# One attention stage: scores of the next head pair ahead of other stages' work, and one reciprocal for two query tiles

## The chip, the cores and the metric

The kernel runs on one core of a Trainium2 chip. The core has a matrix engine (TensorE, PE in the profile; its weight loads are PEld), a vector engine (VectorE, DVE), a scalar engine (ScalarE, ACT), a general engine (GpSimd, POOL) and a queue engine for transfers (SyncE, SP). Each takes its instructions in the order in which they were written for it; semaphores tie the engines together. The metric is the device time of one execution in microseconds (us), the median of several runs.

## The reference, cut to what matters

The program is a chain of four blocks ("macaron": half a feed-forward layer, attention, half a feed-forward layer) on 8 x 512 tokens of 128 features, all in float32. The stage that is changed is the attention of the third block, called L2:

```python
def _L2_attn_ref(x, Wq, Wk, Wv, Wo, bo):
    B, N, D, H, DH = (2, 256, 128, 16, 64)
    b, n, _ = x.shape
    scale = DH ** (-0.5)
    q = (x @ Wq).reshape(b, n, H, DH)
    ...
    bias = slope[:, None, None] * (pos[:, None] - pos[None, :])
    scores = jnp.einsum('bihd,bjhd->bhij', q, k) * scale + bias[None]
    causal = pos[:, None] >= pos[None, :]
    scores = jnp.where(causal[None, None], scores, jnp.float32(-1e+30))
    attn = jax.nn.softmax(scores, axis=-1)
    out = jnp.einsum('bhij,bjhd->bihd', attn, v).reshape(b, n, H * DH)
    return out @ Wo + bo
```

In the chain it stands between two feed-forward layers; the last of L1 and the first of L3 run beside it:

```python
    x = x + 0.5 * _L1_ffn_ref(_layernorm(x, axis=-1), ...)
    x = x + 0.5 * _L2_ffn_ref(_layernorm(x, axis=-1), ...)
    x = x + _L2_attn_ref(_layernorm(x, axis=-1), ...)
    x = x + 0.5 * _L2_ffn_ref(_layernorm(x, axis=-1), ...)
    x = x + 0.5 * _L3_ffn_ref(_layernorm(x, axis=-1), ...)
```

The batch is 8 here, the sequence 512 and there are 16 heads of 64 features.

## The kernel before

`l2_block` (L1642) handles one pair of heads of one batch element at a time; such a pair is called a unit. There are 8 batches x 8 pairs = 64 units, numbered n. The 512 queries of a unit are four tiles i = 0 to 3 of 128 queries. As attention is causal, tile i has 128 (i + 1) keys, and its probabilities stand side by side in one row of 1280 columns from the offsets `OFF`.

For a unit these steps are done, each by a small function that issues instructions and often returns the ACT part to be issued later:

- `project(n)` (L1668): two matmuls give queries and keys of both heads (`pp`), ACT copies them to SBUF (`qk`, L1676), negated and scaled.
- `values(n, half)` (L1679): the value matmuls (`vp`, L1687) and DVE's copy `v` (L1688).
- `score(n, i)` (L1696): one score matmul for each head (`s`, L1706); DVE adds the bias and takes the row minimum in one pass (L1710; as queries are negated, the minimum is the maximum); ACT takes the exponential and, in the same pass, the row sum (L1713). The sum goes to column i of the little tile `sums[n]`.
- `norm(n, *tiles)` (L1736): for each tile named, DVE takes the reciprocal of the two heads' sums (L1740) and multiplies both heads' probabilities (L1743).
- `turn(n, m)` (L1721): PE transposes four 128 x 128 blocks of probabilities (`tp`, L1732), ACT copies them out (`pt`, L1734). Five such calls make up a unit.
- `weigh(n)` (L1745): eight matmuls of probabilities and values (`o`, L1757) and ACT's copy `att` (L1760).
- `leave(b)` (L1762), once for each batch: the output projection (`op`, L1766) and the update of x.

Other stages' work runs in the same loop. `plan` (L331) puts its steps under numbers in the table `todo`, and `works(at)` (L1800) issues what stands under a number. Unit n calls `works(3n)`, `works(3n + 1)` and `works(3n + 2)`: phases 0, 1 and 2. By the numbers given, phase 1 has:

- the update of the two L2 feed-forward steps (`op`, L348, and DVE's `x`, L351; POOL adds the bias);
- the transposes of normalised x for the next batch's projections (`pt`, L314; copy `xta`, L321);
- of the L1 feed-forward layer: the router scores `sp` (L1048), ACT's copy `q` (L1049) and the gelu with its activation table (L1054, L1055), whose next step (L1060 to L1063, ending in ACT's `comp`) is in phase 2; one step each of a long chain of small DVE operations (L1087 to L1091; L1111 to L1115 and L1126); the spline (`pa`, L1138; ACT's copy L1145; eight DVE operations L1148 to L1155), whose next step (a second `pa` and ACT's L1163) is in phase 2;
- of the L3 feed-forward layer: the transposes `pt` with ACT's copy `xt` (L314, L321), whose next step, the routing logits `lp` (L366), is in phase 2; and three of the eight expert steps (`yp`, L384, and four updates of x by DVE, L386);
- one projection of the L3 attention (L1932) with its transfers to and from HBM, and its values (L1953).

In this text a unit is named after such a work: the gelu unit, the route unit, the spline unit, the expert units, the pick unit (L1111 to L1126) and the turn unit (the transposes for the next batch's projections).

PE, ACT and DVE run in the order of the calls in the loop (L1811 on); nothing reorders them. PSUM is split in two: the score tiles `s` have two buffers, and everything else in the loop (`bank`, L1663) shares four buffers named "mm". Which of the four a tile takes is settled when the program is built; a tile's first matmul waits until the last reader of the buffer's former tile is done. In each unit the order is:

1. three of the five `turn` calls of unit n - 1, `project(n + 1)`, `score(n, 2)`, `score(n, 1)`; ACT's copies and exponentials of these and of the two scores that were begun in the unit before are then interleaved;
2. the last two `turn` calls, `norm(n, 3, 0)`, `works(3n)`, `values`, perhaps `leave`;
3. these lines (L1833 to L1843):

```python
                    if two:
                        weigh(n - 2)
                    if here:
                        norm(n, 2, 1)
                    works(3 * n + 1)
                    if -1 <= n and n + 1 < last:
                        late = score(n + 1, 3)
                        late += score(n + 1, 0)
                    if -3 <= n < 5:
                        slopes(n + 3)
                    works(3 * n + 2)
```

`slopes` (L1690) makes the bias of two heads on DVE, in the first units only. The exponentials in `late` are issued in the next unit, after the copies of the first two `turn` calls.

## Time and profile before

| what | value |
|---|---|
| median of 3 runs | 2609.69 us (2609.08 to 2613.6) |
| the profiled execution | 2632.98 us |
| its span, first to last instruction | 2631.2 us |
| mean granted TensorE clock | 0.960 |
| PE busy, share of the span | 2389.5 us, 91% |
| DVE busy | 2024.7 us, 77% |
| ACT busy | 1756.3 us, 67% |
| POOL busy | 1154.0 us, 44% |
| first and last score matmul of the stage (L1706) | 1014.0 and 1848.0 us |

The profile is of one execution, which with profiling on took a little longer than the runs. The span is the time from its first to its last instruction. "Busy" adds up an engine's instructions; matmuls overlap, and their ends are modelled. A row of a time line has the start, the length, the engine, the line of the program, the operation, out<-in by the program's names, the shape and the count of merged instructions; in brackets stands how long the engine had been idle before it and what ended that. A row of the list of groups has busy time and mean length, then the idle time before these instructions. A row of the list of waits has the total, the number and the longest.

### The profile page before, as it was taken

What the parts mean: (1) busy time and instruction counts of PE and PEld (TensorE: products, weight loads), DVE (VectorE), ACT (ScalarE), POOL (GpSimd) and SP (SyncE); (2) the same over time, 40 slices, a digit from 0 to 9 for tenths busy, and PEclk for the clock granted to TensorE, in tenths of its full rate; (3) what the DMA queues carried; (4) which work ended last, traced back from release to release, by engine and by line L of the source; (5) the groups of instructions that cost most, each with busy time, mean ns of one, the idle gap of its engine ahead of it and who ended that gap; (6) DMA issues with size and microseconds to landing.
All of it is one profiled execution on the core that took longest, in us unless ns stands there. A gap on an engine that the chain in (4) does not pass through costs nothing.

```text
span 2631.2 us, 51301 instructions
## 1 busy us (share of the span) xinstructions
PE 2389.5 (91%) x18184; PEld 1427.7 (54%) x18184; DVE 2024.7 (77%) x5597; ACT 1756.3 (67%) x4393; POOL 1154.0 (44%) x2003
## 2 busy tenths in 40 slices
PE   6858756999999998999999999999899999999997
PEld 6537533344444444566565655556565666666664
DVE  5347348888888866878788787877688989898897
ACT  2135134466677666766757676676598999999984
POOL 5655643244454452163452635332234545454443
PEclk9878877799999999999999999999899999999999
DMA  8121340001010100000000000000000000000000
GB/s 270 51 81 30 93 124 1 18 18 27 19 26 19 34 2 4 1 1 1 1 1 1 1 1 1 1 1 9 9 18 9 10 22 22 10 14 22 22 2 13
DMA packets 72962, 66.51 MB, mean 25 GB/s; under 512 B 15675, under 2 KB 62787, under 8 KB 70563
## 3 DMA queue, kind: packets, MB, share of 16 engines
q1 hardware_dynamic: 68096, 54.88, 7.7%
q0 software_dynamic: 3584, 7.58, 1.0%
q8 instruction: 145, 2.38, 0.4%
q10 hardware_dynamic: 1026, 0.78, 0.1%
q14 instruction: 111, 0.90, 0.1%
HBM read 36.47 MB, written 26.80 MB: 24 GB/s over the span
## 4 chain that ended last, share of the span: by engine, by line
PE 62%; DVE 20%; ACT 9%; POOL 4%; issue 3%; DMA 1%; another core or an unknown queue 0%; SPq 0%; POOLq 0%; DVEq 0%; ACTq 0%
PE tp L1476 8%; PE s L1450 6%; PE s L1290 5%; PE o L1757 4%; PE o L1492 4%; PE o L1320 4%; PE s L1706 4%; PE yp L384 3%; ACT e L1713 3%; PE s L1310 3%; DVE nm L1291 3%; DVE nm L1454 3%; PE tp L1732 2%; PE pp L1674 2%; PE hp L684 2%
## 5 line engine op out<-in xcount | busy, mean ns | idle before, releaser
L1461 ACT ACTIVATE e<-s,nm 128x512 f32<-128x512 f32 x512 | 345.4, 689 | 26.0 <-DVE nm L1454 21.4
L1291 DVE TENSOR_REDUCE nm<-s 128x2 f32<-128x1024 f32 x256 | 301.4, 1218 | 75.9 <-PE s L1310 61.0
L1454 DVE TENSOR_REDUCE nm<-s 128x2 f32<-128x1024 f32 x256 | 301.0, 1217 | 29.6 <-PE s L1450 27.7
L1482 ACT ACTIVATE p<-tp 128x512 f32<-128x512 f32 x512 | 279.3, 618 | 61.6 <-PE tp L1476 61.6
L1312 ACT ACTIVATE pr<-s 128x512 f32<-128x512 f32 x512 | 271.6, 600 | 73.1 <-PE s L1310 69.3
L1476 PE MATMUL tp<-cst,e 128*128 128x128 f32 x2048 | 294.3, 282 | 15.2 <-DVE rs L1467 7.9
L1476 PEld LDWEIGHTS tp<-cst,e 128*128 128x128 f32 x2048 | 221.5, 142 | 153.0 <-issue 86.8
L1470 POOL TENSOR_SCALAR e<-e,rs 128x512 f32<-128x512 f32 x114 | 200.1, 1755 | 229.8 <-DVE rs L1467 191.3
L1290 PE MATMUL s<-k,q 32*128 32x512 f32 x1024 | 279.2, 657 | 18.0 <-DVE nm L1291 14.6
L1310 PE MATMUL s<-q,k 32*128 32x512 f32 x1024 | 290.4, 627 | 5.4 <-DVE at L1333 4.4
L1713 ACT ACTIVATE e<-e,m 128x512 f32<-128x512 f32 (+3 forms) x512 | 286.1, 570 | 12.6 <-DVE m L1710 12.5
L1710 DVE CUSTOM_DVE_ANT_0 e<-s,bias 128x512 f32<-128x512 f32 (+3 forms) x512 | 220.1, 485 | 92.9 <-PE s L1706 92.4
L219 POOL TENSOR_TENSOR d<-st 128x4 f32<-128x4 f32 (+3 forms) x90 | 19.7, 218 | 554.2 <-DVE st L215 356.9
L1734 ACT COPY pt<-tp 128x512 f32<-128x512 f32 x320 | 174.5, 590 | 90.1 <-PE tp L1732 90.1
L386 DVE SCALAR_TENSOR_TENSOR x<-yp,sel,x 128x128 f32<-128x128 f32 x512 | 177.9, 348 | 39.7 <-PE yp L384 26.6
L1470 DVE TENSOR_SCALAR e<-e,rs 128x512 f32<-128x512 f32 x398 | 195.5, 521 | 9.1
L1743 DVE TENSOR_SCALAR e<-e,rc 128x512 f32<-128x512 f32 (+3 forms) x512 | 190.0, 416 | 9.1
L1732 PE MATMUL tp<-cst,e 128*128 128x128 f32 x1280 | 170.9, 278 | 9.8 <-ACT pt L1734 4.0
L1450 PE MATMUL s<-k,q 32*128 32x512 f32 x1024 | 174.8, 651 | 5.1 <-ACT e L1461 2.6
L1706 PE MATMUL s<-qk 64*128 64x512 f32 (+3 forms) x1024 | 173.6, 457 | 2.0 <-DVE m L1710 1.4
L1492 PE MATMUL o<-p,va 128*32 128x128 f32 x4096 | 165.8, 277 | 2.9 <-ACT p L1482 2.9
L1732 PEld LDWEIGHTS tp<-cst,e 128*128 128x128 f32 x1280 | 139.2, 141 | 48.5 <-issue 13.3
(467 smaller groups left out, 4848.0 us busy)
## 6 DMA issues: line engine op xcount, KB each, us to landing
yd<-z SPq DMA_DIRECT2D x8, 1024.0 KB
r<-yd SPq DMA_DIRECT2D x32, 256.0 KB
sk<-pu SPq DMA_DIRECT2D x16, 256.0 KB
k<-sk SPq DMA_DIRECT2D x60, 64.0 KB
w<-in_l_w SPq DMA_DIRECT2D x14, 256.0 KB
xd<-wqkv SPq DMA_DIRECT2D x12, 256.0 KB
x<-in_x SPq DMA_DIRECT2D x8, 256.0 KB
up<-in_l_up SPq DMA_DIRECT2D x8, 256.0 KB
```

The lines of the kernel that those rows point to most:

```text
L1290: nc.tensor.matmul(s[:, jj, :], lhsT=q[cut, g, i * P : (i + 1) * P], rhs=k[cut, g, :], start=True, stop=True)
L1291: nc.vector.tensor_reduce(nms[b, g // 2][:, i, 2 * h : 2 * h + 2, g % 2], s, AX.X, ALU.max, negate=True)
L1310: nc.tensor.matmul(s, lhsT=k[cut, g, kt * P : (kt + 1) * P], rhs=q[cut, g, :], start=True, stop=True)
L1450: nc.tensor.matmul(s[:, jj, :], lhsT=q[cut, g, i * P : (i + 1) * P], rhs=k[cut, g, :], start=True, stop=True)
L1454: nc.vector.tensor_reduce(nm, scores[n, h], AX.X, ALU.max, negate=True)
L1461: nc.scalar.activation(e, s[:, jj, :], AF.Exp, bias=nm[:, jj : jj + 1], accum_out=sm[:, jj : jj + 1])
L1470: (nc.gpsimd if h and jj and n >= 14 else nc.vector).tensor_scalar(e, e, rc[:, jj : jj + 1], None, ALU.mult)
L1476: nc.tensor.transpose(tp[:, kt, :], probs[n][j][:, kt * P : (kt + 1) * P], self.ident)
L1482: nc.scalar.activation(p, turns[n].pop(0), AF.Exp)
L1706: nc.tensor.matmul(s[:, jj, 0:w], lhsT=qs[n][cut, i * P : (i + 1) * P], rhs=ks[n][cut, 0:w], start=True, stop=True)
L1713: outs.append(lambda e=e, jj=jj: nc.scalar.activation(e, e, AF.Exp, bias=mins[n][:, jj, i : i + 1], scale=-1.0, accum_out=sums[n][:, jj, i ...
L1732: nc.tensor.transpose(tp[:, k, :], block(n, jj, i, kt), self.ident)
```

## The change

Two things are changed in `l2_block`.

The row sums of a unit no longer stand in the order of the tiles but as `SUM` says: tiles 3, 0, 2, 1 in columns 0 to 3. So the two tiles of each `norm` call stand next to each other, and one reciprocal over 2 heads x 2 tiles takes the place of two over 2 heads each. The multiplications stay as they are.

In the third part of a unit, `norm(n, 2, 1)` is written ahead of `weigh(n - 2)`, and the two scores of the next unit ahead of `works(3n + 1)`. So the order becomes: normalise, weigh, the next unit's two scores (matmuls and minima), other stages' work of phase 1, slopes, other stages' work of phase 2.

```diff
-        OFF = (0, 128, 384, 768)
+        OFF, SUM = (0, 128, 384, 768), (1, 3, 2, 0)
...
-                        e, e, AF.Exp, bias=mins[n][:, jj, i : i + 1], scale=-1.0, accum_out=sums[n][:, jj, i : i + 1]))
+                        e, e, AF.Exp, bias=mins[n][:, jj, i : i + 1], scale=-1.0, accum_out=sums[n][:, jj, SUM[i] : SUM[i] + 1]))
...
             def norm(n, *tiles):
 
-                for i in tiles:
-                    rc = wk.tile([P, 2], F32, tag="rc", name="rc", bufs=4)
-                    nc.vector.reciprocal(rc, sums[n][:, :, i])
+                rc = wk.tile([P, 2, 2], F32, tag="rc", name="rc", bufs=4)
+                nc.vector.reciprocal(rc, sums[n][:, :, SUM[tiles[0]] : SUM[tiles[0]] + 2])
+                for k, i in enumerate(tiles):
                     for jj in range(2):
                         e = es[n][:, jj, OFF[i] : OFF[i] + P * (i + 1)]
-                        nc.vector.tensor_scalar(e, e, rc[:, jj : jj + 1], None, ALU.mult)
+                        nc.vector.tensor_scalar(e, e, rc[:, jj, k : k + 1], None, ALU.mult)
...
+                    if here:
+                        norm(n, 2, 1)
                     if two:
                         weigh(n - 2)
-                    if here:
-                        norm(n, 2, 1)
-                    works(3 * n + 1)
                     if -1 <= n and n + 1 < last:
                         late = score(n + 1, 3)
                         late += score(n + 1, 0)
+                    works(3 * n + 1)
                     if -3 <= n < 5:
                         slopes(n + 3)
                     works(3 * n + 2)
```

## The prediction

> **What bounds the kernel now.** I read the page first (busy time by engine), then busy time in a window around the changed stage, then its waits, then the time line of TensorE (PE), ScalarE (ACT) and VectorE (DVE) over the eight units from 1353.1 to 1464.1 us. The stage's first score matmul is at 1014.0 us and its last at 1848.0; I take 1010 to 1860. Only there does the order change: on POOL and SP, and on every engine before and after this stage, the built programs have the same instructions in the same order.

> Window view; the columns are length, then busy us of PE, its weight loads, DVE, ACT, POOL:

> ```profile
> 1010.00:1860.00 850.00, 809.92 (x4803) 495.68 (x4802) 671.92 (x2596) 597.55 (x1665) 339.51 (x745) 1.00 0.01 3
> ```

> PE is idle for 850.00 - 809.92 = 40.1 us, DVE for 178.1, ACT for 252.5. The matmuls stand end to start, so PE sets the pace, and all that a better order can bring here is part of those 40.1 us. A new order of PE's own work costs nothing in itself; it costs where PE then has to wait.

> The stage repeats every eight units: the output projection (L1766) comes at 1242.21, 1353.14, 1464.07, 1575.00, 1685.95, so a period is 110.9 us. PE's time line in one period ("idle before" in brackets, with its releaser):

> ```profile
> 1382.99 1.12 PE L1674 MATMUL pp<-xta,wqkv 128*128 128x512 f32 x2 [1.07 <-ACT pt L1734]
> ...
> 1414.61 0.66 PE L314 MATMUL pt<-cst,xn 128*128 128x128 f32 x4
> 1415.19 1.35 PE L1706 MATMUL s<-qk 64*128 64x512 f32 x8
> 1416.47 1.06 PE L366 MATMUL lp<-gw,xt 128*128 128x8 f32 x8
> ...
> 1431.53 1.35 PE L1706 MATMUL s<-qk 64*128 64x384 f32 x8 [0.23 <-DVE m L1710]
> 1434.20 0.44 PE L1131 MATMUL tp<-cst,k 128*128 128x128 f32 x2 [0.30 <-ACT qk L1676]
> 1436.35 2.37 PE L1757 MATMUL o<-pt,v 128*64 128x512 f32 x16 [0.54 <-ACT pt L1734]
> ...
> 1444.71 0.66 PE L1732 MATMUL tp<-cst,e 128*128 128x128 f32 x4 [0.41 <-ACT k L1163]
> ...
> 1458.06 1.98 PE L1674 MATMUL pp<-xta,wqkv 128*128 128x512 f32 x4
> ```

> The same period on ACT:

> ```profile
> 1378.41 0.40 ACT L1049 COPY q<-sp 128x288 f32<-128x288 f32 x1 [1.42 <-PE sp L1048]
> 1378.82 1.28 ACT L1055 ACT_TABLE_LOAD   x1
> 1380.12 0.31 ACT L1055 ACTIVATE q<-q 128x128 f32<-128x128 f32 x1
> 1381.98 0.49 ACT L1063 ACTIVATE comp<-q,cb 128x4 f32<-128x4 f32 x2 [1.55 <-DVE q L1061]
> ...
> 1415.38 0.61 ACT L321 ACTIVATE xt<-pt 128x512 f32<-128x512 f32 x1
> ...
> 1430.90 0.72 ACT L1713 ACTIVATE e<-e,m 128x512 f32<-128x512 f32 x1 [1.14 <-DVE m L1710]
> ...
> 1443.52 1.15 ACT L1163 ACTIVATE k<-pa,q 128x128 f32<-128x128 f32 x4 [2.88 <-PE pa L1138]
> ```

> And DVE (the expert updates L386 and the reciprocals are what to look at):

> ```profile
> 1455.00 0.15 DVE L1740 RECIPROCAL rc<-sm 128x2 f32<-128x2 f32 x1
> 1455.18 0.65 DVE L1743 TENSOR_SCALAR e<-e,rc 128x256 f32<-128x256 f32 x2
> 1455.76 1.50 DVE L386 SCALAR_TENSOR_TENSOR x<-yp,sel,x 128x128 f32<-128x128 f32 x4
> 1457.17 0.68 DVE L1710 CUSTOM_DVE_ANT_0 e<-s,bias 128x512 f32<-128x512 f32 x1
> ```

> **Prices used throughout.** A pair of score tiles holds PE for 1416.47 - 1415.19 = 1.28 us. DVE can begin its four minimum passes (L1710) 1.18 us after the scores start (1378.24 to 1379.42 in the gelu unit) and they take 1.64 (1443.08 to 1444.72, the next start). Four expert updates take 1.42 to the next start, 1.50 to their end.

> **The change, part by part.**

> *Reciprocals.* 256 of 0.159 us become 128; each new one covers twice the columns (by the 128x32 one of L1088, 0.353, two more columns are about 0.013). DVE is spared 256 x 0.159 - 128 x 0.172 = 18.7 us, nearly all beside PE's work: DVE already waits 92.4 us for score matmuls. It reaches the path where PE waits for a normalised tile: 1.87 and 1.21 us at 1022.7 and 1031.9 and 0.57 at 1853.1, each shortened by two omitted instructions of 0.19 (0.15 and its gap, rows above): -1.1 us. The joint reciprocal waits for the later of two exponentials; where that binds (after 1390.3, the first pair was scaled while the second was awaited) DVE is 0.8 late, to 1393.25, but the scores it reads next are not there before 1393.67.

> *Normalising ahead of weighing.* One is DVE's, the other PE's and ACT's: the order on no engine changes. Nothing.

> *Scores ahead of the other stages' work.* Every such work of phase 1 comes 1.28 us later on PE and 1.64 later on DVE; the minima come earlier by what stood before them. Unit by unit:

> Route unit (1412 on). Before, the scores stood between the transposes pt and the routing matmuls lp, and hid the copy xt. Now pt starts at 1414.61 + 1.28 = 1415.89, the copy 0.77 after it as before (1415.38 - 1414.61), ends at 1417.27, and lp starts at about 1417.3 instead of 1416.47: +0.8. Behind lp on PE stand the next unit's transposes, on which ACT waits. Seven such units; in the last one L1953's vp (1.0 us) stands between, as the cover: 6 x 0.8 = +4.8.

> Gelu unit (1374 on). The router scores sp come 1.28 later, so copy q, table load and gelu end at 1380.43 + 1.28 = 1381.71. L1060 and L1061 used to wait for the minima (until 1381.07), and now for gelu; with 0.46 + 0.42 and the gaps comp starts at 1382.65 instead of 1381.98. The pt copies stand behind comp, and PE's 1.07 wait is for them: +0.67. From there ACT is continuous to the wait at 1390.18, so nothing gives it back. 6 x 0.67 = +4.0.

> Pick unit and spline unit (1424, 1436). In the first, the minima no longer stand behind six instructions of L1111 to L1126; ACT's 1.14 wait goes and with it PE's 0.23 + 0.30 + 0.54 = 1.07. In the second the direction: scores now at 1437.58 (1438.65 - 1.07), minima from 1438.76 to 1440.40, updates to 1441.82, the spline's eight (1.76) to 1443.58. ACT's L1163 needs the last of them: 1443.62, it was 1443.52. So the pair gives back what it gains: +0.1, six times: +0.6. Without the first unit's gain it would be +1.2 each.

> Expert units. In the changed program the unit's first projection pp takes a PSUM buffer that the first expert update still reads; 18 units have such a wait, none before (transposes and later tiles had it). Around 1458: DVE is free 0.38 sooner, at 1455.38; minima to 1457.02, update to 1458.52, pp at 1458.58 instead of 1458.06: +0.5, 6 x = +3.0. In the third of the three units (1366) the same sum ends at 1366.94, before pp's 1367.17: nothing, with 0.2 to spare. In the first (spline) the update ends with the transposes.

> Turn unit (1401). PE's 0.14 wait goes, six times: -0.8.

> Other moved work is covered: x L351 is read next 1.8 us later at 1396.22 and ends at 1396.1; the projection at 1830.03 sends its transfer 1.28 later, but that of the other half, whose source is ready only at 1841.54, is the later one anyway. POOL's operations stay in their order and wait 245.9 us for DVE already.

> **Sum.** 4.8 + 4.0 + 0.6 + 3.0 - 1.1 - 0.8 = +10.5 us. The profiled execution took 2632.98 us (span 2631.2), 23.3 above the median of the runs, 2609.69; I add the same to both: span about 2641.7, time 2620. From both sides, each term: route 0 to 5.6; gelu 0 to 4.0; pick and spline -6.4 (all of 1.07, nothing late) to 7.2 (6 x 1.2); experts 0 to 5.6 (0.5 plus the 1366 unit's margin missed by 0.4); gains -3 to 0.

> [...]

> **Rivals.**
> 1. Faster, one mechanism: the earlier minima free ACT in the pick unit, and the spline's chain does not bind. For it: ACT's 12.5 us of waiting for minima. Against: the spline's last result (L1155, to 1443.17) comes only 0.35 us before L1163 starts. It pays -6.4 - 1.1 - 0.8 = -8.3 and decides if route, gelu and experts together lose less than that, as when PE's later waits absorb them: 2601.
> 2. No change: PE's work is the same and gains meet losses: 2610. For it: 95% busy; against: waits now exposed are not among the old ones.
> 3. Slower still: the pick unit gains nothing and all bank waits bite: 5.6 + 4.0 + 7.2 + 5.6 = 22 us, 2632. Against: DVE has six instructions fewer before those minima.

> **How the numbers follow.** The forecast 0.55, rival 3 0.10, rival 2 0.16, rival 1 0.19. This kernel's measurement tells 0.2%, 5.2 us, from no change. So faster 0.19, same 0.16, slower 0.65. The forecast's own range is 2615 to 2626; across the cases 2602 to 2631.

> **What would show it.** Route unit: lp with an idle time of 0.8 before it, for ACT xt. Gelu unit: the second pp waiting 1.7. Pick unit: no waits at L1706, L1131, L1757. Expert unit: pp waiting 0.5 for DVE x. PE's idle time in the stage near 51 us, not 40; 128 reciprocals. It is wrong if PE's idle time falls, or if the time moves outside this stage.

## The result and the profile after

| what | before | after |
|---|---|---|
| median of the runs beside each other | 2610.15 us | 2618.6 us |
| ratio | | 1.0039, 95% interval 1.0030 to 1.0048 |
| first to last score matmul of the stage | 833.98 us | 843.41 us |
| stage, from first to last weighing | | +9.25 us |
| DVE busy in the execution | 2024.7 us | 2006.2 us |

The change makes the kernel 8.45 us slower by the medians, 0.3% to 0.4%. (The ratio is not formed from the medians, whose quotient is 1.0032; its interval holds both.) The profiled execution of after has the shorter span (2612.4 us), because the part ahead of the stage happened to take 26 us less in it: the first score matmul comes at 987.7 us and not at 1014.0. So only the stage is compared below.

Busy time in a window around the stage, columns as before (length; PE, its weight loads, DVE, ACT, POOL):

```profile
984.00:1834.00 850.00, 796.83 (x4750) 494.69 (x4751) 649.52 (x2450) 588.35 (x1649) 339.00 (x745) 0.99 0.01 3
```

PE is now idle for 850.00 - 796.83 = 53.2 us (40.1 before), and DVE has less to do. The waits of PE in that window, after (what waited and for what; total, times, longest):

```profile
PE pp L1674 <- ACT pt L1734: 16.1, 6, 3.0
PE tp L1732 <- ACT k L1163: 9.8, 5, 2.0
PE o L1757 <- ACT pt L1734: 7.8, 12, 0.9
PE tp L1732 <- ACT pt L1734: 4.3, 14, 0.8
PE lp L366 <- ACT xt L321: 4.1, 6, 0.7
```

Before, the same list has 8.8 for the first, 2.1 for the second, 7.7 for the third and nothing for `lp`. PE's time line in one period of after shows where they stand:

```profile
1360.35 2.08 PE L1674 MATMUL pp<-xta,wqkv 128*128 128x512 f32 x2 [2.98 <-ACT pt L1734]
...
1393.78 1.06 PE L366 MATMUL lp<-gw,xt 128*128 128x8 f32 x8 [0.69 <-ACT xt L321]
...
1407.96 1.35 PE L1706 MATMUL s<-qk 64*128 64x384 f32 x8
...
1412.35 1.08 PE L1757 MATMUL o<-pt,v 128*64 128x512 f32 x4 [0.93 <-ACT pt L1734]
...
1422.06 0.66 PE L1732 MATMUL tp<-cst,e 128*128 128x128 f32 x4 [1.95 <-ACT k L1163]
...
1435.12 0.66 PE L1732 MATMUL tp<-cst,e 128*128 128x128 f32 x4 [0.29 <-ACT pt L1734]
```

These are the gelu unit (2.98 us of waiting, 1.07 before), the route unit (0.69, none before), the pick unit (one wait of 0.93 where there were three, of 0.23, 0.30 and 0.54), the spline unit (1.95, was 0.41) and the expert unit (0.29, none before).

A wait alone does not tell what a unit costs, as matmuls overlap (in after the projection's two from 1360.35 take 2.08 us, and the scores start at 1362.36). So I measured each unit from its first weighing matmul (L1757) to the next unit's, in the trace of each kernel, and took the difference to before. The sums over the units of a kind (eight, for expert seven), in us:

| unit | predicted | after | order alone | reciprocals alone | pick and turn alone |
|---|---|---|---|---|---|
| gelu | +4.0 | +6.7 | +1.9 | 0.0 | 0.0 |
| route | +4.8 | +2.4 | +3.0 | +3.5 | +2.0 |
| pick | } +0.6 | -5.8 | -4.4 | -2.3 | -6.1 |
| spline | } | +8.1 | +9.8 | 0.0 | 0.0 |
| expert (the one behind spline) | +3.0 | +2.5 | +1.5 | 0.0 | 0.0 |
| turn | -0.8 | -3.4 | +1.0 | -0.9 | -3.2 |
| the two others | 0 | -1.3 | -1.2 | +0.3 | +0.3 |
| all | +10.5 with -1.1 for the reciprocals | +9.25 | +11.6 | +0.6 | -7.1 |

The last three columns are from experiments 1 to 3. Each column is one execution; that of after was the fastest of its ten runs.

### The profile page after: what moved, and what is told of

The parts are those of the page before. It is cut to its first block, busy times and chain, and to the rows that moved or that the text cites. A ratio compares the mean times of both kernels' runs of the same rounds, so it can differ in the third digit from the quotient of the medians.

```text
span 2612.4 us, 51166 instructions
## 1 busy us (share of the span) xinstructions
PE 2375.1 (91%) x18184; PEld 1427.1 (55%) x18184; DVE 2006.2 (77%) x5469; ACT 1754.9 (67%) x4393; POOL 1152.0 (44%) x2003
## 4 chain that ended last, share of the span: by engine, by line
PE 64%; DVE 20%; ACT 8%; POOL 4%; issue 2%; DMA 1%; SPq 0%; ACTq 0%; DVEq 0%; POOLq 0%
PE tp L1476 8%; PE s L1450 6%; PE s L1290 5%; PE o L1757 5%; PE s L1706 4%; PE o L1492 4%; PE o L1320 4%; PE tp L1732 3%; PE s L1310 3%; DVE nm L1291 3%; PE yp L384 3%; DVE nm L1454 3%; PE pp L1674 3%; ACT e L1713 2%; PE hp L684 2%
## 5 line engine op out<-in xcount | busy, mean ns | idle before, releaser
L1710 DVE CUSTOM_DVE_ANT_0 e<-s,bias 128x512 f32<-128x512 f32 (+3 forms) x512 | 220.3, 486 | 134.7 <-PE s L1706 134.7
L1713 ACT ACTIVATE e<-e,m 128x512 f32<-128x512 f32 (+3 forms) x512 | 286.4, 571 | 4.7 <-DVE m L1710 4.2
L1734 ACT COPY pt<-tp 128x512 f32<-128x512 f32 x320 | 173.9, 590 | 76.8 <-PE tp L1732 76.8
L386 DVE SCALAR_TENSOR_TENSOR x<-yp,sel,x 128x128 f32<-128x128 f32 x512 | 177.3, 348 | 27.4 <-PE yp L384 13.7
L1732 PE MATMUL tp<-cst,e 128*128 128x128 f32 x1280 | 170.9, 278 | 19.5 <-ACT k L1163 9.8
L1743 DVE TENSOR_SCALAR e<-e,rc 128x512 f32<-128x512 f32 (+3 forms) x512 | 174.6, 407 | 4.5
L1706 PE MATMUL s<-qk 64*128 64x512 f32 (+3 forms) x1024 | 176.6, 464 | 0.7 <-ACT qk L1676 0.7
L1732 PEld LDWEIGHTS tp<-cst,e 128*128 128x128 f32 x1280 | 140.9, 142 | 56.7 <-ACT e L1713 11.9
```

Source lines behind the costliest of these rows:

```text
L1706: nc.tensor.matmul(s[:, jj, 0:w], lhsT=qs[n][cut, i * P : (i + 1) * P], rhs=ks[n][cut, 0:w], start=True, stop=True)
L1713: outs.append(lambda e=e, jj=jj: nc.scalar.activation(e, e, AF.Exp, bias=mins[n][:, jj, i : i + 1], scale=-1.0, accum_out=sums[n][:, jj, S ...
L1732: nc.tensor.transpose(tp[:, k, :], block(n, jj, i, kt), self.ident)
```

## The experiments

Ten kernels were run, on three chips. Two of these ran the kernel before in 2641 and 2644 us instead of 2610, so ratios are compared; each is to the kernel before on the same chip.

**1 to 3: the two halves of the change, and the units that gained.** The first kernel has the old order and the joint reciprocals, the second the new order and the old reciprocals. In the third the loop chooses by the unit:

```diff
+                    first = n % 8 in (5, 7)
+                    if not first:
+                        works(3 * n + 1)
                     if -1 <= n and n + 1 < last:
                         late = score(n + 1, 3)
                         late += score(n + 1, 0)
-                    works(3 * n + 1)
+                    if first:
+                        works(3 * n + 1)
```

> The order of the calls is the old one everywhere; only the reciprocals are joined. Theory of PE's waits: PE sets the pace and the reciprocals stand ahead of PE's work at three places only, so -0.3 to -1.1 us against the kernel before (ratio 0.9996 to 0.9999); DVE's busy time falls by some 18 us and its idle time in the stage grows by as much. Rival, DVE sets the pace: -18.7 us (0.993).

> The new order of the calls with the old reciprocals, 256 of them. If the order alone costs the time: +8.5 to +9.5 us against before (1.0033 to 1.0036). Rival: the joint reciprocal, which waits for the later of two exponentials, has a part in the loss; then this is less than +6 us (1.002).

> The next unit's scores come first in the pick and the turn units alone; in the six other units of eight the other stages' work comes first as before; reciprocals joined. Theory of PE's waits, unit by unit: the pick units' -5.5 us and the turn units' -3.4 us, read in the changed kernel's trace, are kept and nothing is lost: -7 to -9 us against before, about 2602 (0.997), without half-clock windows in the stage. Rival, the gains are given back at the next wait (spline unit, gelu unit): within 2 us of before.

| kernel | median | ratio | 95% interval |
|---|---|---|---|
| reciprocals alone | 2609.44 | 0.9996 | 0.9987 to 1.0005 |
| order alone | 2621.42 | 1.0043 | 1.0030 to 1.0057 |
| pick and turn alone | 2600.60 | 0.9967 | 0.9957 to 0.9978 |

Sparing DVE 18.7 us (its busy time goes from 2024.7 to 2006.0 us) brings nothing that can be measured, so DVE does not set the pace. The whole loss is the order's. And the order is worth having in two units of eight: with the other six as before, the kernel is 9.2 us faster than before by the medians, and no later unit takes the gain back (gelu and spline 0.0).

The route unit was not as expected: the reciprocals alone, in the old order, make it 0.66 us longer in five of its eight turns. DVE and then PE in that kernel:

```profile
1389.69 0.18 DVE L1739 RECIPROCAL rc<-sm 128x4 f32<-128x4 f32 x1 [1.27 <-ACT e L1713]
...
1394.09 0.19 DVE L417 TENSOR_TENSOR lg<-lp,lm 128x32 f32<-128x32 f32 x1
...
1392.24 1.51 PE L1732 MATMUL tp<-cst,e 128*128 128x128 f32 x12
1394.43 1.96 PE L1674 MATMUL pp<-xta,wqkv 128*128 128x512 f32 x4 [0.68 <-DVE lg L417]
```

The joint reciprocal waits 1.27 us for the later of two exponentials. Behind it in DVE's order stand the multiplications, five operations of the L1 layer, the minima and then L417, the last reader of `lp`'s buffer. That buffer is the next projection's, so PE waits 0.68 us. In before DVE and PE stood so, with a wait of 0.23 us and none for PE:

```profile
1414.84 0.17 DVE L1740 RECIPROCAL rc<-sm 128x2 f32<-128x2 f32 x1 [0.23 <-ACT e L1713]
...
1418.58 0.19 DVE L417 TENSOR_TENSOR lg<-lp,lm 128x32 f32<-128x32 f32 x1
...
1418.91 1.96 PE L1674 MATMUL pp<-xta,wqkv 128*128 128x512 f32 x4
```

**4: is it the lower clock?** In after, PE's wait of 2.98 us is followed by a stretch of granted clock near one half (0.54 over the 3.60 us shown below). The kernel fills the wait:

```diff
-                    nc.tensor.matmul(pp, lhsT=wq[:, m, at : at + P], rhs=xts[b], start=True, stop=True)
+                    for _ in range(3 if m == 0 and n % 8 == 5 and n < 48 else 1):
+                        nc.tensor.matmul(pp, lhsT=wq[:, m, at : at + P], rhs=xts[b], start=True, stop=True)
```

> The changed kernel, and the first projection matmul (pp, 512 columns) of the unit in which PE waits 2.98 us is issued three times instead of once, the same result written thrice: PE works through some 2.2 us of the wait. Theory of the clock: the half-clock windows that follow these waits vanish and each gives back some 1.2 us: +3 to +5 us against before instead of +8.5. Rival, the lower clock in the records has no part in the time: +8.5 us as the changed kernel, or more if the two matmuls do not fit into the wait.

2618.72 us, ratio 1.0044 (1.0029 to 1.0059): no better than after. For the gelu units the theory of the clock falls. Windows of after and of the filled kernel in the same gelu unit (the third number from the end is the granted clock):

```profile
1360.40:1364.00 3.60, 3.60 (x10) 1.49 (x10) 0.04 (x1) 3.57 (x8) 0.00 (x0) 0.54 0.00 0
```

```profile
1361.00:1368.00 7.00, 5.17 (x26) 2.92 (x26) 4.12 (x18) 6.97 (x18) 0.08 (x1) 1.00 0.00 0
```

The clock is 0.54 in the one and 1.00 in the other, and yet the unit is 1.75 us longer than before in both. ACT is busy for 3.57 of 3.60 and 6.97 of 7.00 us: here ACT's late copies set the end, and PE has time to spare, at half clock too. Only in the last of these units, where half clock lasted 6.83 us in after, does after need 0.5 us more (2.27 against 1.75). What remains is why ACT is late by 1.75 us and not by the 0.67 of the prediction. The order alone had 0.67 to 0.68, four times.

**5: a collision of DVE and POOL.** DVE's L1060, ahead of ACT's comp, and POOL's L349, in before and then in after:

```profile
1381.07 0.42 DVE L1060 TENSOR_TENSOR q<-q,cw 128x256 f32<-128x256 f32 x1
...
1381.55 1.27 POOL L349 TENSOR_TENSOR x<-x,bh 128x512 f32<-128x512 f32 x1
```

```profile
1357.35 1.51 DVE L1060 TENSOR_TENSOR q<-q,cw 128x256 f32<-128x256 f32 x1 [1.33 <-ACT q L1055]
...
1357.31 1.26 POOL L349 TENSOR_TENSOR x<-x,bh 128x512 f32<-128x512 f32 x1
```

In after POOL starts 0.04 us ahead of DVE, and the DVE operation takes 1.51 us, not 0.42. With the order alone L1060 starts 0.12 to 0.16 us ahead of L349 and takes 0.42. The experiment moves POOL by one small operation, done twice in the gelu units (lines behind it shift by one):

```diff
-        pool.tensor_tensor(rs, r0, h, ALU.mult)
+        for _ in range(2 if getattr(self, "gelu", False) else 1):
+            pool.tensor_tensor(rs, r0, h, ALU.mult)
...
+                    self.gelu = n % 8 == 3 and n > 8
                     works(3 * n)
+                    self.gelu = False
```

> The changed kernel, and in the gelu units POOL does one small operation of 0.20 us twice (L230, the same result), so that its 128x512 addition L349 starts some 0.28 us later and no longer 0.03 us ahead of DVE's L1060. Theory of the collision: whichever of the two starts first holds the other up; L1060 goes back from 1.51 to 0.42 us in four gelu units, each of which gives back 1.09 us, although DVE and PE have no instruction more or less: -4.4 us against the changed kernel, so about +4 us against before. Rival, the length of L1060 does not reach PE: no difference to the changed kernel (+8.5).

```profile
1389.57 0.42 DVE L1061 TENSOR_TENSOR q<-q,cw 128x256 f32<-128x256 f32 x1 [1.33 <-ACT q L1056]
...
1389.81 1.30 POOL L350 TENSOR_TENSOR x<-x,bh 128x512 f32<-128x512 f32 x1
```

DVE comes first now and takes 0.42; the four gelu units are 0.66 to 0.67 us longer than before and no longer 1.75 to 2.27. So the collision is shown in its place (0.42 us for 1.51). The time did not follow: 2649.94 us beside 2641.45, ratio 1.0037 (1.0023 to 1.0051), no different from after. The theory's +4 us would be 1.0015, outside this interval, so it is not shown that the time of a run falls by these 4.4 us. In the profiled execution the stage is 843.15 us: the gelu units give back 4.6 us, but two spline units had a stretch of half clock (3.4 us), and the turn units lost 1.0 us (below).

**6 to 8: three kinds of unit undone, each by itself.** The kernel of after, with `first = n % 8 != 0`, `6` or `1` in the loop of experiment 3.

> The changed kernel, but in the spline units the other stages' work stands ahead of the next unit's scores as before. Theory: the spline units' +1.26 us each (PE's wait for L1163, 1.95 instead of 0.41) vanish and the pick units ahead of them keep their -0.94: -7 to -8 us against the changed kernel, so +0.5 to +1.5 against before. Rival, my prediction's reading, in which the pair of units can only give back what it gains: then the pick units lose their gain with it and this is +7 to +8.5.

> The changed kernel, but in the route units the other stages' work stands ahead of the next unit's scores as before. My prediction's reading: the wait of 0.69 us of lp for ACT's xt is what the route unit loses, so it gains 4.1 us: +4.4 against before. Rival: the joint reciprocal costs the route unit 0.4 to 0.66 us in either order (it does so in the runs with the old order there), so undoing the order gains nothing: +8.5 to +10 us against before.

> The changed kernel, but in the one expert unit that became 0.41 us longer the other stages' work stands ahead of the next unit's scores as before. Theory: those six units are again as long as before and no other unit changes: -2.5 us against the changed kernel, about +6 against before, and PE's wait of 0.29 us of the transposes (tp) for ACT's pt is gone. Rival, another unit takes the loss up: +8.5.

| old order in | ratio | 95% interval | that unit, against after |
|---|---|---|---|
| spline | 1.0016 | 1.0004 to 1.0029 | -1.26 in five, -1.65 in the first; pick units unchanged |
| route | 1.0031 | 1.0016 to 1.0046 | 0.00 in five, -0.55 in the seventh |
| expert | 1.0037 | 1.0022 to 1.0052 | -0.42, -0.40, -0.43, -0.42, -0.40, -0.40 |

Spline is the largest loss: undone, 1.0016 instead of 1.0039. By the medians, +4.5 us lies between the theory's +0.5 to +1.5 and the rival's +7 to +8.5, and the interval touches both; the trace decides, for there the pick unit ahead of it keeps its gain. The route unit gains nothing from the old order (+9.9 us by the medians, as the rival had it): there PE waits 0.42 us for L417 instead of 0.69 for `xt`. The expert unit gives back its six times 0.41 and no other unit takes it up in the trace, but the time of that kernel doesn't show it: +9.8 us by the medians, where about +6 was expected. Its profile has two half-clock stretches in spline units, 3.4 us, which the profile of after has not.

**9 and 10: the version that beats both.** Scores first in pick and turn units, and in the route unit the reciprocals of tiles 2 and 1 apart, so that DVE need not wait for the later exponential:

```diff
-                nc.vector.reciprocal(rc, sums[n][:, :, SUM[tiles[0]] : SUM[tiles[0]] + 2])
+                apart = tiles[0] == 2 and n % 8 == 6
+                if not apart:
+                    nc.vector.reciprocal(rc, sums[n][:, :, SUM[tiles[0]] : SUM[tiles[0]] + 2])
                 for k, i in enumerate(tiles):
+                    if apart:
+                        nc.vector.reciprocal(rc[:, :, k], sums[n][:, :, SUM[i]])
```

> As the run with scores first in the pick and turn units alone (2600.6 us), and in the route unit the second normalising call takes its two reciprocals apart again, 8 of 128 joint ones. Theory: there the joint one waits for the later exponential, DVE's L417 comes late and PE waits 0.42 us for its buffer; apart, five units give back 0.4 us: 2598.6 us, 0.9957 to 0.9960 of before. Rival, the wait moves on and nothing is gained: 2600.6.

> As the run with scores first in the pick and turn units and two single reciprocals in the route unit (0.9958 of before), and the scores also come first in the two units behind the gelu and the first expert unit, where the changed kernel's units were 0.08 and 0.20 us shorter. Theory of units that can be summed: 1.4 us less, 0.9950 to 0.9955 of before. Rival, a buffer that the expert update still reads (my prediction's term; six units have such a wait in this order) takes it back: 0.996 or more.

The first: 2631.61 beside 2641.45 us, ratio 0.9958 (0.9946 to 0.9970), as expected. PE's row in the route unit, which in the third experiment had waited 0.42 us for L417:

```profile
1424.82 1.51 PE L1732 MATMUL tp<-cst,e 128*128 128x128 f32 x12
1426.30 1.96 PE L1674 MATMUL pp<-xta,wqkv 128*128 128x512 f32 x4
```

No wait, and the five units are 0.44 to 0.45 us shorter each. The second has 0.9938 (0.9920 to 0.9956), below the 0.9950 to 0.9955 expected. The intervals overlap, and by the units of the two traces they are equal (-9.36 and -9.32 us from first to last weighing): what two kinds of unit gain, gelu and turn units lose. Units can't be summed that far. Either is some 0.4% to 0.6% faster than before, and so faster than both kernels of this case.

## Why the prediction was right, and where not

**Time and sign** held: +8.45 us against +10.5. That the total came so near is partly luck, as the errors of its terms cancel. The gelu units cost 2.7 us more than their term, and lie outside its bounds of 0 to 4.0; the pair of pick and spline cost 1.8 more; route cost 2.4 less, turn 2.6, the two other kinds 1.3 and expert 0.5 less.

**"PE sets the pace"** held in that the joint reciprocals alone changed the time by -0.3 us, within its error; the rival of experiment 1, 18.7 us from DVE's relief, is refuted by the same run. PE's idle time went to 53 us (51 predicted), but idle time is no measure of what an order costs. Between the stage's first and last score matmul it went from 37.0 to 51.7 us, 14.7 more, while this stretch grew by 9.4 us; with scores first in pick and turn alone it is 36.5 us, hardly less, and the stretch is 7.1 us shorter. PE's busy time changed too, with 4727 or 4728 matmuls in each: 797.0 us before, 791.7 after, 790.4 with pick and turn alone. So "all that a better order can bring here is part of those 40.1 us" does not hold.

**Spline and pick** were right in mechanism and nearly in size: +1.26 and -0.94 for +1.17 and -1.07. The sum missed because the pair does not just give back what it gained: it loses 0.32 more each time, and the first spline unit lost 1.65. They don't hang together either, as experiment 6 shows. The chain is the one foreseen; DVE and then ACT in a spline unit of after:

```profile
1415.83 0.69 DVE L1710 CUSTOM_DVE_ANT_0 e<-s,bias 128x512 f32<-128x512 f32 x1 [0.54 <-PE s L1706]
...
1417.48 1.50 DVE L386 SCALAR_TENSOR_TENSOR x<-yp,sel,x 128x128 f32<-128x128 f32 x4
...
1420.52 0.23 DVE L1155 TENSOR_SCALAR q<-q,os 128x4 f32<-128x4 f32 x1
...
1420.87 1.14 ACT L1163 ACTIVATE k<-pa,q 128x128 f32<-128x128 f32 x4 [2.95 <-DVE q L1155]
```

The minima and the updates now stand ahead of the spline's last result, ACT idles 2.95 us for it, and PE behind ACT 1.95.

The pick unit's gain also arose otherwise: the waits only fell from 1.07 to 0.93, as the one for ACT's `pt` grew; the rest is matmuls that follow each other more closely where no wait stands between. "A new order of PE's own work costs nothing in itself" was too simple: the stretch from the first score matmul behind the projection to the weighing took 1436.35 - 1431.53 = 4.82 us before and 1412.35 - 1407.96 = 4.39 after, 0.43 less, with 0.84 us of waits in the former and 0.93 in the latter.

**Gelu.** The step "L1060 and L1061 ... with 0.46 + 0.42 and the gaps" took L1060's duration from the trace of before, where POOL's addition starts behind it. It does so still with the order alone, and there the term is right to a hundredth in four units (the first two don't lose). With both halves of the change POOL starts 0.03 to 0.04 us ahead of DVE, and 1.08 us or more are added four times. This was the failing step, as far as the units of the traces tell. The trace of before had a warning: in one early gelu unit, at 1158.15 us, L1060 took 1.47 us.

**Route.** The wait of `lp` came as predicted, 0.69 for 0.8. But the unit's cost is 0.40, and taking the wait away brings nothing: the joint reciprocal's delay stands behind it. The step that failed is that of the reciprocals: "where that binds ... the scores it reads next are not there" looked at one place only. In the route unit L417 is what comes late, and with it PE's buffer. The two costs don't add: 0.53 for the order alone, 0.66 for the reciprocals alone, 0.40 for both. The gain of 1.1 us by the reciprocals did not come: up to the first weighing the stage is 0.05 us shorter.

**Expert.** +0.41 for +0.5, but by another wait. `pp` does not wait for DVE's x; a transpose `tp` waits 0.29 us for ACT's `pt`. Two matmul groups `yp` now stand next to each other ahead of three groups `tp`, all in the four shared buffers. That a buffer is late is right; which one was wrong.

**Turn.** -0.8 predicted, -3.4 found. Four units gain 0.74 each, and only 0.15 of that is the wait named. With pick and turn alone a unit gains 0.53, again with 0.15 of waits; the rest is matmuls that follow each other more closely. The order alone gains nothing here (-0.11 to +0.05 in five units, +1.30 in the first) and the reciprocals alone 0.14 to 0.37, so the gain needs both. In the filled kernel four such units gain only 0.33 to 0.35. There DVE's L1091 takes 1.15 us, and POOL's addition to x (L1768 there) started 0.2 us before it; in after it takes 0.40, and that addition starts 0.8 us behind it. But its length doesn't explain the difference: with only the spline order undone L1091 takes 0.19 us in four turn units, and they gain 0.39 to 0.41. What the other 0.3 to 0.4 us hang on stays open; no run was made for it.

## What to carry to other kernels

Judge an order unit by unit, and let the loop choose: the same move gained 0.94 us where six DVE operations that nobody waited for had stood ahead of the scores' minima and lost 1.26 where another stage's chain on DVE led back to PE. When two operations are joined into one, look at everything that stands behind it on its engine, not at what it saves. And take a duration from the trace only after looking at what the other engines did at that moment: a shift of 0.2 us between two engines took L1060 from 0.42 to 1.51 us.

## What the runs showed of the hardware

**DVE's L1060 and POOL's L349 hold each other up.** In the kernel with only the spline order undone, L1060 and L349 start within 0.01 us of each other, and the outcome goes both ways:

```profile
1391.81 0.43 DVE L1060 TENSOR_TENSOR q<-q,cw 128x256 f32<-128x256 f32 x1 [1.33 <-ACT q L1055]
...
1391.81 1.55 POOL L349 TENSOR_TENSOR x<-x,bh 128x512 f32<-128x512 f32 x1
...
1613.42 1.53 DVE L1060 TENSOR_TENSOR q<-q,cw 128x256 f32<-128x256 f32 x1 [1.33 <-ACT q L1055]
1613.41 1.26 POOL L349 TENSOR_TENSOR x<-x,bh 128x512 f32<-128x512 f32 x1
```

Either DVE takes 0.43 and POOL 1.55, or POOL 1.26 and DVE 1.53: the loser takes longer by most of the winner's length (0.29 of 0.43, 1.11 of 1.26). Where the starts lay further apart, the one that started first kept its length: in after POOL 1.26, 0.04 us ahead of DVE, and with the order alone DVE 0.43, 0.15 us ahead of POOL, which then took 1.39. It is not so with every POOL instruction: in before, in four gelu units, the last one of L275 started 0.39 to 0.40 us ahead of L1060 and lasted 0.79 to 0.80, and L1060 took its 0.42 all the same. Why the two differ was not shown.

**Half clock after waits of 2 to 3 us.** In the stage of after the granted clock fell to 0.50 five times, each time within 0.4 us of the end of a PE wait of 2.27 to 2.98 us, four times for 3.41 us and once for 6.83. It does not fall after each wait of some 2 us. With the order alone, two spline units with the same wait of 1.96 us:

```profile
1205.90:1209.20 3.30, 3.30 (x10) 1.08 (x8) 0.27 (x1) 2.66 (x9) 0.00 (x0) 0.57 0.00 0
1320.20:1323.50 3.30, 3.30 (x20) 2.00 (x19) 1.84 (x10) 3.30 (x12) 0.00 (x0) 1.00 0.00 0
```

The first has clock 0.57 and ten matmuls in 3.30 us, the second 1.00 and twenty; the first unit is 1.65 us longer. In after, none of the five spline waits of 1.95 us was followed by half clock; in before, a wait of 2.12 us was (it ended at 1161.11) and one of 2.40 us was not (1060.63). In the gelu units, where ACT sets the end, a single stretch of 3.41 us cost nothing: 1.75 us longer than before with it in after, and 1.75 without it in the filled kernel.
